# Deformable convolution on one core: halves of the first places, scales by DMA, and ScalarE weighting one of four neighbours

## The chip, the cores and the metric

The kernel runs on one core of a Trainium2 chip. The metric is the device time of one execution in microseconds (us). A core has five engines that run their own instruction streams and meet through semaphores: TensorE (PE, with its weight loads PEld), VectorE (DVE), ScalarE (ACT), GpSimd (POOL) and SyncE (SP, which here only issues DMAs).

## The reference

Four "metaformer" layers follow each other on x of shape (4, 128, 64, 64): each is a convolution-like mixer on a normalised x, added to x, and then a token mixer, added again. The change touches one of these eight steps, the mixer of layer 1: a modulated deformable 3x3 convolution. Cut to that:

```python
off  = conv2d(xn, w_off, b_off)                 # xn: x normalised over channels; 2 offsets per tap
mask = sigmoid(conv2d(xn, w_mod, b_mod))        # 9 taps
py, px = h + ky + dy, w + kx + dx               # where tap (ky, kx) of pixel (h, w) looks
y0, x0 = floor(py), floor(px); wy, wx = py - y0, px - x0
v00, v01, v10, v11 = xn at (y0,x0), (y0,x0+1), (y0+1,x0), (y0+1,x0+1)   # zero outside the image
sampled = (v00*(1-wy)*(1-wx) + v01*(1-wy)*wx + v10*wy*(1-wx) + v11*wy*wx) * mask
x = x + einsum('bckhw,ock->bohw', sampled, weight) + bias
```

## The kernel before

x stays in SBUF for the whole kernel as `xs`, 128 channels on the partitions, 4096 pixels per image (batch). An image is 8 chunks of 512 pixels, each 4 tiles of 128. The stage of interest is `deformable`, between the recurrence of layer 0 and the expert choice of layer 1.

Two taps of the nine (`HATS`) are computed without gathering, by hat functions (`hats`, whose steps lay work on every engine except GpSimd; `fold` prepares its matrices). The other seven (`BY_ASK`) gather. For each chunk and tap the four tiles are done in two pairs, so a chunk is 14 pairs, an image 112 and the stage 448. `taken` serves a pair: two indirect DMAs on GpSimd (L998) bring, for each of 128 pixels, the four neighbours' 128 channels (512 floats) from a table in DRAM into a buffer `dcn_g` (8 buffers); then one VectorE product (L1006) multiplies all of it, 1024 columns, by the weights. The weights lie in PSUM as `near_w`, copied there once a chunk (L1160). `joined` lets TensorE transpose the four weighted neighbours of a tile into the same PSUM columns, so that they add up: eight transposes a pair (L1015). `turn_back` copies the result to SBUF on ScalarE (L1120), `convolve` multiplies it by the tap's weights (L1127), and `finish` adds the chunk to `xs` (L1135).

Before an image can gather it needs its table and its places, which `plan(b)` prepares: the pixels are centred (L753, L756), their variances found (L759, L765), the reciprocal deviations made (`inverted`, L777), and each chunk is scaled (`scaled`: a matmul L792 spreads a row of deviations over the partitions, L801 multiplies). `turned` transposes the normalised rows and writes them to the table by SP DMAs (L818, L820, L827, L829). `offsets` convolves for offsets and mask, two halves of an image (L840, L849, L858). `places` turns them into indices (L915 to L944) and weights (L953 to L978) for the whole image, 288 columns a partition.

The order on TensorE, ScalarE, VectorE and GpSimd is the order of the program text (`manual_schedule`); each engine runs its stream in order. `plan` is a generator. For image 0 it runs to its end before the first gather. For image b+1 it is the side work of image b: every `step`, one per pair, advances it by one `yield`, every fifth step by two; what is left at the end of an image is run out before the next begins. `at(lag, ...)` defers work by so many steps: a pair's joins come two steps after its product.

Of the kernel before, what the change touches and what calls it, by code (L numbers as in the profile page):

```python
# [10 lines left out]

# [6 lines left out]
F32 = mybir.dt.float32  # L18
# [10 lines left out]
P = 128  # L29
# [563 lines left out]
class Sampling:  # L593
# [8 lines left out]
    def __init__(self, net, one, dram):  # L602
# [6 lines left out]
        self.tables = [dram.tile([SIDE * SIDE + 1, 2, P], F32, name=f"dcn_table{b}") for b in range(B)]  # L609
        zero = one.tile([SIDE + 1, 2 * P], F32, name="dcn_zero")  # L610
# [84 lines left out]
def deformable(net, sampling):  # L695
# [19 lines left out]
    with ExitStack() as ctx:  # L715
# [5 lines left out]
        far = one.tile([P, B + 1], F32, name="dcn_far")  # L721
# [14 lines left out]
        def plan(b):  # L736
# [4 lines left out]
            def bank(tag="pd" if b else "pt"):  # L741
                return ps.tile([P, CH], F32, name=f"dcn_{tag}", tag=tag, bufs=BANKS[tag])
# [45 lines left out]

            def scaled(c):
                rows = slice(32 * (c % 4), 32 * (c % 4) + 32)  # L790
                pb = bank()
                nc.tensor.matmul(  # L792
                    pb,
                    net.ident[rows, rows.start : rows.start + 1].to_broadcast([32, P]),
                    rstds[c // 4][rows],
                    start=True,
                    stop=True,
                )
                yield
                d = inside(c)  # L800
                nc.vector.tensor_mul(d, d, as_shape(pb, d))  # L801
                yield
# [75 lines left out]
            for c in half:  # L878
                yield from scaled(c)
            if b == 0:  # L880
                yield from abreast(
                    one_by_one(*(turned(c) for c in half)),
                    one_by_one(inverted(1), *(scaled(4 + c) for c in half)),
                )
                yield from abreast(
                    one_by_one(*(turned(4 + c) for c in half)),
                    one_by_one(offsets(0), offsets(1), places(b, off)),
                )
                return
            yield from turned(0)  # L890
            yield from turned(1)
            yield from inverted(1)
            yield from turned(2)
            yield from turned(3)
            for c in half:
                yield from scaled(4 + c)
# [6 lines left out]
            yield from places(b, off)  # L903

        def places(b, off):

            frac, row = [], new("row")
            hat = sb.tile([P, NT, NH, PICKED], F32, name="dcn_hat", tag="dcn_hat", bufs=1)
            apart = sb.tile([P, NT, NH, 1], F32, name="dcn_apart", tag="dcn_apart", bufs=1)
            pieces = sb.tile([P, NT, NH * PICKED, 3], BF16, name="dcn_pieces", tag="dcn_pieces")  # L910
            at = slice(H0, H0 + NH)
            for axis in range(2):
                pos, low, lowi, over = new("pos"), new("low"), new("lowi", I32), new("over")
                frac.append(new(f"frac{axis}"))
                nc.vector.tensor_add(pos, grids[axis], off[:, :, axis : 18 : 2])  # L915
                if axis == 0:
                    nc.vector.tensor_sub(apart[:, :, :, 0], pos[:, :, at], grids[0][:, :, at])
                    yield
                    nc.vector.tensor_reduce(
                        far[:, b : b + 1],  # L920
                        apart.rearrange("p t k o -> p (t k o)"),
                        AX.X,
                        ALU.max,
                        apply_absolute_value=True,
                    )
                else:
                    nc.vector.tensor_copy(hat[:, :, :, 0], pos[:, :, at])
                nc.vector.tensor_scalar(pos, pos, -1.0, float(H), op0=ALU.max, op1=ALU.min)
                yield

                nc.vector.tensor_copy(lowi, pos)
                nc.vector.tensor_copy(low, lowi)
                yield
                nc.vector.tensor_tensor(over, low, pos, ALU.is_gt)
                nc.vector.tensor_sub(low, low, over)
                yield
                nc.vector.tensor_sub(frac[axis], pos, low)
                if axis == 0:
                    nc.vector.tensor_scalar(row, low, float(SIDE), float(SIDE + 1), op0=ALU.mult, op1=ALU.add)
                else:  # L940
                    nc.vector.tensor_add(row, row, low)
                yield
            idx = new("idx", I32)
            nc.vector.tensor_copy(idx, row)  # L944
            ly, lx = frac
            mask, lo, hi = new("pos"), new("low"), new("over")
            w = new("w")
# [4 lines left out]
            shape = [P, NT, NH, PICKED - 1]  # L952
# [25 lines left out]
            nc.vector.tensor_mul(wq[1], hi, lx)  # L978
            made[b] = (sampling.squares(tables[b]), idx, w, pieces, turns[b])
# [11 lines left out]
        near_w = ps.tile([P, 2, Q4, KK, 4], F32, name="dcn_near_w", bufs=1)  # L991

        def taken(rows, idx, c, k, i):


            g = sb.tile([P, 2, 4 * P], F32, name="dcn_g", tag="g", bufs=GATHERED)
            for t in range(2):
                nc.gpsimd.indirect_dma_start(  # L998
                    out=g[:, t, :],
                    out_offset=None,  # L1000
                    in_=rows,
                    in_offset=bass.IndirectOffsetOnAxis(ap=idx[:, Q4 * c + i + t, k : k + 1], axis=0),
                )
            near = g.rearrange("p t (q c) -> p t q c", c=P)
            by = near_w[:, c % 2, i : i + 2, k, :].unsqueeze(3).to_broadcast([P, 2, 4, P])
            nc.vector.tensor_mul(near, near, by)  # L1006
            return near

        def joined(pt, i, near):

            if i == 0:
                pt[0] = ps.tile([P, CH], F32, name="dcn_pt", tag="pt", bufs=BANKS["pt"])
            for t in range(2):
                for q in range(4):
                    nc.tensor.matmul(  # L1015
                        pt[0][:, (i + t) * P : (i + t + 1) * P],
                        near[:, t, q, :],
                        net.ident,
                        is_transpose=True,
                        start=i + t + q == 0,  # L1020
                        stop=i + t + q == 6,
                        skip_group_check=True,
                    )
# [79 lines left out]
        with tc.manual_schedule(engines=ORDERED):  # L1103
# [44 lines left out]
            for b in range(B):  # L1148
                for _ in side:
                    pass  # L1150
                side = plan(b + 1) if b + 1 < B else iter(())
# [7 lines left out]
                for c in range(NCH):  # L1159
                    nc.vector.tensor_copy(near_w[:, c % 2], w[:, Q4 * c : Q4 * c + Q4])  # L1160
                    po = {}
                    busy.append(hats(b, c, po, pieces, turned))
                    if c == 2:
                        keep(b, idx, w)
                    if b == 0 and c < B:
                        nc.sync.dma_start(sampling.kept[c].rearrange("c p t -> p c t"), as_chunks(net.xs[:, c, :]))
                    for k in BY_ASK:
                        pt = {}
                        for i in range(0, 4, 2):
                            at(2, joined, pt, i, taken(rows, idx, c, k, i))  # L1170
                            if i:
                                at(4, turn_back, k, pt, po, b, c)
                            step()
            while later:
                step()
            nc.vector.tensor_reduce(far[:, B : B + 1], far[:, 0:B], AX.X, ALU.max)
            pt = ps.tile([P, CH], F32, name="dcn_pt", tag="pt", bufs=BANKS["pt"])
            nc.tensor.transpose(pt[0:1, 0:P], far[:, B : B + 1], net.ident)
# [1453 lines left out]
```

## Time and profile before

| | |
|---|---|
| median of 3 executions | 6042.37 us (6040.1 to 6043.02) |
| the profiled execution | 6034.38 us, its span 6032.6 us |
| mean granted TensorE clock | 0.975 |
| busy over the span | PE 5684.2, DVE 4380.3, ACT 3365.4, POOL 2057.2 us |
| first and last start of a gather (L998) | 1310.9 and 2445.4 us |
| gathers | 896, 851.3 us busy |

A row of a group reads: line, engine, operation, tiles out<-in, shapes, count | busy us, mean ns of one | idle time of the engine just before them, and what ended it. In a table of windows each engine has its busy time and, in brackets, its instructions; PEclk is the granted clock, DMA the busy share of the 16 DMA engines. In a timeline the columns are the start and the duration in us, and in square brackets the idle time before.

### The profile page before, as it was taken

To read this page: it belongs to the slowest core of one execution; us is meant where nothing else is said; L and a number is where in the kernel's file an instruction comes from. 1 tells how busy PE (TensorE), PEld (TensorE's weight loads), DVE (VectorE), ACT (ScalarE), POOL (GpSimd) and SP (SyncE) were. 2 spreads that over 40 slices of the span, in tenths; PEclk is the share of its full clock that TensorE was granted. 3 is DMA by queue.
4 is the path that set the end of the run, shared out by engine and by line. 5 is a ranking of instruction groups with operands and counts; after the bars stand their busy time and mean duration, and the time that the engine had idled before them with its cause. 6 is when DMAs were issued, how large, how long until landed. Compare 5 with 4: busy or idle time off the path is not lost. (4 is left out here: it accounts for less than half of the span.)

```text
span 6032.6 us, 97814 instructions
## 1 busy us (share of the span) xinstructions
PE 5684.2 (94%) x39896; PEld 2250.6 (37%) x39927; DVE 4380.3 (73%) x4783; ACT 3365.4 (56%) x4213; POOL 2057.2 (34%) x2015
## 2 busy tenths in 40 slices
PE   8999999889999988879979999999999999999799
PEld 2222222346667766433333222322232223222233
DVE  6888887456767676456446888888888888888666
ACT  4444444333323322521336888888888888999421
POOL 3898897027777777200010111111111111111000
PEclk9999999989999999979989999999999999999899
DMA  6434432057777777550274666656665666666200
GB/s 215 98 74 90 89 76 47 1 150 231 217 229 217 228 221 210 167 183 0 88 266 111 133 155 146 138 130 154 146 141 128 151 148 142 133 131 131 60 25 27
DMA packets 273274, 818.39 MB, mean 136 GB/s; under 512 B 42644, under 2 KB 100392, under 8 KB 226728
## 3 DMA queue, kind: packets, MB, share of 16 engines
q0 software_dynamic: 109568, 505.75, 35.2%
q1 hardware_dynamic: 163240, 306.20, 17.5%
q8 instruction: 320, 5.24, 0.4%
q14 instruction: 146, 1.20, 0.1%
HBM read 416.71 MB, written 93.13 MB: 85 GB/s over the span
## 5 line engine op out<-in xcount | busy, mean ns | idle before, releaser
L2035 ACT ACTIVATE att_ex<-att_sc,att_shift 128x1024 f32<-128x1024 f32 x2048 | 2141.8, 1111 | 281.3 <-PE att_sc L2031 165.1
L2066 DVE TENSOR_TENSOR att_dve<-att_dve,att_ex 128x2048 f32<-128x2048 f32 x704 | 1631.5, 2317 | 154.0 <-ACT att_ex L2035 129.2
L2031 PE MATMUL att_sc<-att_q,att_k 32*128 32x512 f32 x8192 | 1280.8, 640 | 0.0
L2047 PE MATMUL att_pv<-att_ex,att_vals 128*32 128x512 f32 x8192 | 1092.2, 605 | 0.0
L998 POOL DMA_INDIRECT dcn_g<-dcn_table,dcn_idx x896 | 851.3, 950 | 354.3 <-issue 150.8
L412 DVE SCALAR_TENSOR_TENSOR inv_prod<-inv_pk,bspan,inv_seen 128x512 f32<-128x512 f32 (+1 forms) x1120 | 774.5, 743 | 141.4 <-PE inv_pk L399 141.0
L410 POOL TENSOR_TENSOR inv_prod<-inv_seen,inv_prod 128x512 f32<-128x512 f32 (+1 forms) x672 | 837.5, 1273 | 95.2 <-ACT inv_prod L409 95.2
L2064 POOL DMA_DIRECT2D att_dma<-att_ex x224 | 192.5, 859 | 1965.1 <-ACT att_ex L2035 1738.6
L409 ACT ACTIVATE inv_prod<-inv_pk,bspan 128x512 f32<-128x512 f32 (+1 forms) x672 | 436.1, 682 | 504.9 <-PE inv_pk L399 493.7
L2031 PEld LDWEIGHTS att_sc<-att_q,att_k 32*128 32x128 f32 x8192 | 423.5, 183 | 656.5 <-issue 416.8
L1006 DVE TENSOR_TENSOR dcn_g<-dcn_g,dcn_near_w 128x1024 f32<-128x1024 f32 x448 | 538.9, 1214 | 164.9 <-DMA dcn_g<-dcn_table,dcn_idx 153.4
L399 PE MATMUL inv_pk<-inv_red,wtap 32*96 32x512 f32 (+1 forms) x3584 | 512.1, 637 | 7.3 <-DVE wtap L377 7.3
L1015 PE MATMUL dcn_pt<-ident,dcn_g 128*128 128x128 f32 x3584 | 472.9, 276 | 34.0 <-ACT dcn_st L1120 16.4
L1015 PEld LDWEIGHTS dcn_pt<-ident,dcn_g 128*128 128x128 f32 x3584 | 419.1, 142 | 206.9 <-issue 116.1
L421 PE MATMUL inv_out<-inv_prod,inv_fold 96*32 96x512 f32 (+1 forms) x3584 | 478.6, 606 | 8.5 <-DVE xs L429 8.5
L2047 PEld LDWEIGHTS att_pv<-att_ex,att_vals 128*32 128x32 f32 x8192 | 161.8, 108 | 752.2 <-issue 727.0
L399 PEld LDWEIGHTS inv_pk<-inv_red,wtap 32*96 32x96 f32 (+1 forms) x3584 | 131.9, 171 | 386.2 <-DVE inv_prod L412 362.5
L1034 ACT ACTIVATE dcn_fold<-dcn_pf,dcn_turn 128x256 f32<-128x256 f32 x128 | 60.2, 473 | 366.0 <-PE dcn_pf L1030 366.0
L1120 ACT COPY dcn_st<-dcn_pt 128x512 f32<-128x512 f32 x224 | 129.9, 580 | 241.0 <-PE dcn_pt L1015 241.0
L1127 PE MATMUL dcn_out<-dcn_st,dcn_wk 128*128 128x512 f32 x448 | 236.0, 609 | 25.0 <-DVE xs L1135 23.1
L2536 PE MATMUL top_po<-top_xg,top_we 128*128 128x512 f32 x512 | 233.3, 599 | 0.0
L1054 DVE TENSOR_TENSOR dcn_square<-dcn_hx,dcn_by 128x512 f32<-128x512 f32 x192 | 130.0, 677 | 115.4 <-PE dcn_by L1040 75.5
(442 smaller groups left out, 5358.1 us busy)
## 6 DMA issues: line engine op xcount, KB each, us to landing
att_dma<-att_ex POOLq DMA_DIRECT2D x224, 1024.0 KB, 7.0
inv_seen<-inv_image SPq DMA_DIRECT2D x256, 266.0 KB, 9.1
moe_w<-in_L_ffn_weight SPq DMA_DIRECT2D x64, 1024.0 KB, 14.2
att_dma<-att_ex SPq DMA_DIRECT2D x32, 1024.0 KB, 9.0
att_dve<-att_dma POOLq DMA_DIRECT2D x32, 1024.0 KB
moe_table<-moe_xt SPq DMA_DIRECT2D x64, 288.0 KB, 2.8
dcn_table<-dcn_xt SPq DMA_DIRECT2D x32, 512.0 KB, 4.8
dcn_g<-dcn_table,dcn_idx POOLq DMA_INDIRECT x896, 3.7
```

Of the source, the lines that this page charges most:

```text
L399: nc.tensor.matmul(pk[0:m], wtap[half][rg, i, blk], red[rg, h * CH : (h + 1) * CH], start=True, stop=True)
L409: nc.scalar.activation(prod[0:m, h], pk[0:m], AF.Identity, bias=by)
L410: nc.gpsimd.tensor_mul(of, view, of)
L412: nc.vector.scalar_tensor_tensor(out=of, in0=as_shape(pk[0:m], of), scalar=by, in1=view, op0=ALU.add, op1=ALU.mult)
L421: nc.tensor.matmul(po[CR * blk : CR * (blk + 1), h, :], fold[0:m], prod[0:m, h, :], start=unit == 0, stop=unit == UNITS - 1,)
L998: nc.gpsimd.indirect_dma_start(out=g[:, t, :], out_offset=None, in_=rows, in_offset=bass.IndirectOffsetOnAxis(ap=idx[:, Q4 * c + i + t, k ...
L1006: nc.vector.tensor_mul(near, near, by)
L1015: nc.tensor.matmul(pt[0][:, (i + t) * P : (i + t + 1) * P], near[:, t, q, :], net.ident, is_transpose=True, start=i + t + q == 0, stop=i + ...
L2031: nc.tensor.matmul(pes[h // 2][:, h % 2, :], ks[r, t * P : (t + 1) * P], q[r], start=True, stop=True)
L2035: nc.scalar.activation(ex[:, 2 * two : 2 * two + 2, :], pes[two], AF.Exp, bias=shifts[g][:, two : two + 1],)
L2047: nc.tensor.matmul(block["pv"][r], vals[:, t, r], ex[:, h, :], start=t == 0, stop=t == NT - 1)
L2066: nc.vector.tensor_add(block[who], block[who], ex)
```

## The change

- Image 0's places are made in halves. The first half (chunks 0 to 3) follows the first half of the offsets; the second offsets and the second half of the places become side work of image 0, ahead of `plan(1)`, and must be done by chunk 3. `places` takes a slice `part` and a column of `far` for it; `places_held` makes the tiles.
- For images 1 to 3 the row of deviations is written to DRAM (`spread_out`) and read back spread over 128 partitions (`way`), in place of the matmul in `scaled`. The order of `plan` changes: `inverted(1)` comes first, the second half is scaled earlier.
- Of a tile's four neighbours, the first is weighted by ScalarE into one of three slots of PSUM, which lie in one bank with `near_w`. VectorE multiplies the last two neighbours as before (512 columns), and then, in `added`, forms second x weight + slot, per tile. Three transposes a tile remain. `near_w` holds two weights instead of four, once instead of twice.

The core of the diff (places' statements, which only gain the slices, are left out):

```diff
+            front = [b == 0]
+            def bank(tag=None):
+                tag = tag or ("pt" if front[0] else "pd")
...
+            def spread_out(h):
+                nc.sync.dma_start(sampling.spread[b][4 * h : 4 * h + 4, :], rstds[h][0:P:32])
+                yield
+                for c in range(4 * h, 4 * h + 2):
+                    way(c)
+                    yield
+            def way(c):
+                by = ways[c] = sb.tile([P, CH], F32, name="dcn_way", tag="ln_sq", bufs=4)
+                nc.sync.dma_start(by, sampling.spread[b][c : c + 1, :].to_broadcast([P, CH]))
             def scaled(c):
+                if b:
+                    pb = ways.pop(c)
+                else:
...
                 yield
                 d = inside(c)
                 nc.vector.tensor_mul(d, d, as_shape(pb, d))
+                if b and c % 4 < 2:
+                    way(c + 2)
                 yield
...
             yield from inverted(0)
             if b == 0:
...
-                    one_by_one(offsets(0), offsets(1), places(b, off)),
+                    one_by_one(offsets(0), places(b, off, held, slice(0, NT // 2), 0)),
                 )
+                front[0] = False
+                rest.append(one_by_one(offsets(1), places(b, off, held, slice(NT // 2, NT), B)))
                 return
+            yield from spread_out(0)
+            yield from inverted(1)
+            for c in half:
+                yield from scaled(c)
+            yield from spread_out(1)
             yield from turned(0)
             yield from turned(1)
-            yield from inverted(1)
+            for c in half:
+                yield from scaled(4 + c)
             yield from turned(2)
...
-        near_w = ps.tile([P, 2, Q4, KK, 4], F32, name="dcn_near_w", bufs=1)
+        shared = ps.tile([P, CH], F32, name="dcn_near_w", bufs=1)
+        near_w = shared[:, 0 : Q4 * KK * 2].rearrange("p (i k q) -> p i k q", k=KK, q=2)
+        first = shared[:, P:CH].rearrange("p (s c) -> p s c", c=P)
+        taking = [0]
...
-            by = near_w[:, c % 2, i : i + 2, k, :].unsqueeze(3).to_broadcast([P, 2, 4, P])
-            nc.vector.tensor_mul(near, near, by)
+            slots = [(taking[0] + t) % 3 for t in range(2)]
+            taking[0] += 2
+            for t in range(2):
+                nc.scalar.activation(
+                    first[:, slots[t], :], near[:, t, 0, :], AF.Copy, scale=w[:, Q4 * c + i + t, k, 0:1]
+                )
+            by = near_w[:, i : i + 2, k, :].unsqueeze(3).to_broadcast([P, 2, 2, P])
+            nc.vector.tensor_mul(near[:, :, 2:], near[:, :, 2:], by)
+            at(1, added, w, c, k, i, near, slots)
             return near
+        def added(w, c, k, i, near, slots):
+            for t in range(2):
+                nc.vector.scalar_tensor_tensor(
+                    out=near[:, t, 1, :], in0=near[:, t, 1, :], scalar=w[:, Q4 * c + i + t, k, 1:2],
+                    in1=first[:, slots[t], :], op0=ALU.mult, op1=ALU.add,
+                )
         def joined(pt, i, near):
-                for q in range(4):
+                for q in range(1, 4):
...
-                side = plan(b + 1) if b + 1 < B else iter(())
+                side = chain(rest[0] if b == 0 else (), plan(b + 1) if b + 1 < B else ())
...
                 for c in range(NCH):
-                    nc.vector.tensor_copy(near_w[:, c % 2], w[:, Q4 * c : Q4 * c + Q4])
+                    if b == 0 and c == NCH // 2 - 1:
+                        for _ in rest[0]:
+                            pass
+                    nc.vector.tensor_copy(near_w, w[:, Q4 * c : Q4 * c + Q4, :, 2:])
```

## The prediction

> **What bounds the kernel now.** The change touches only the deformable convolution, so I read the page for its groups, then its four batches as windows, then the wait list of the line that gathers, then the timelines of GpSimd and of the prelude. Four windows, cut at the first gather of each batch; batches 1 and 3:
>
> ```profile
> core 0: us, PE busy (x) PEld busy (x) DVE busy (x) ACT busy (x) POOL busy (x), PEclk, DMA share, GB/s
> ...
> 1596.00:1882.00 286.00, 272.37 (x1822) 200.25 (x1829) 199.95 (x248) 90.21 (x169) 212.59 (x225) 0.99 0.75 224
> ...
> 2166.00:2446.00 280.00, 241.19 (x1568) 189.52 (x1575) 173.34 (x177) 70.26 (x129) 211.78 (x225) 0.96 0.71 211
> ```
>
> TensorE looks like the limit, 95% busy in batch 1. But batch 3, which has no next batch to prepare and leaves TensorE at 86%, is only 6 us shorter. GpSimd, 75% busy in both, is the engine to look at. The gathering line, with its idle time by releaser (us, times), and its timeline:
>
> ```profile
> L998 POOL DMA_INDIRECT dcn_g<-dcn_table,dcn_idx x896: 940/946/1294, 1310.9 to 2445.4; - x180
> ...
>   issue: 150.8, 495
>   DVE dcn_idx L944: 70.1, 1
> ...
>   DVE dcn_g L1006: 33.1, 90
>   PE dcn_pt L1015: 27.9, 73
> ```
>
> ```profile
> 2201.69 0.95 POOL L998 DMA_INDIRECT dcn_g<-dcn_table,dcn_idx  x1 [0.30 <-issue]
> 2202.94 0.95 POOL L998 DMA_INDIRECT dcn_g<-dcn_table,dcn_idx  x1 [0.30 <-issue]
> ```
>
> Each gather takes 0.946 us and 0.304 us of gap, also where it waits for nothing ("issue": 150.8/495 = 0.305). That is a period of 1.25 us, 2.50 us for a pair, and nothing on GpSimd shortens it. 896 gathers at 1.251 us are 1120.9 us; from the first start to the last the trace has 1134.5 us for 895 periods. The surplus is 15.1 us and can be named: waits for VectorE's product 33.1 - 90 x 0.304 = 5.7; for TensorE's joins 27.9 - 73 x 0.304 = 5.7; gathers longer than the median 851.3 (page) - 896 x 0.946 = 3.7. So GpSimd's pace bounds the stage, and TensorE adds some 11 us. The other two places where this stage can give or lose time are its start, 70.1 us of GpSimd waiting for the first index, and the seams between batches, which cost nothing now (1595.13 to 1596.38, one period).
>
> **The change, part by part.**
>
> *First places in halves.* The prelude on VectorE:
>
> ```profile
> 1291.90 0.80 DVE L858 COPY dcn_off<-dcn_pt 128x108 f32<-128x108 f32 x4 [15.66 <-PE dcn_pt L853]
> 1302.36 0.80 DVE L858 COPY dcn_off<-dcn_pt 128x108 f32<-128x108 f32 x4 [9.66 <-PE dcn_pt L853]
> 1303.20 0.46 DVE L915 TENSOR_TENSOR dcn_pos<-dcn_at,dcn_off 128x288 f32<-128x288 f32 x1
> ...
> 1310.32 0.31 DVE L944 CAST dcn_idx<-dcn_row 128x288 int32<-128x288 f32 x1
> ```
>
> The first half needs only the offsets ready at 1292.7. The chain L915 to L944 takes 7.43 us at 288 columns. At 144 its nine two-input operations save some 0.15 us each (0.46 at 288 against 0.23 at 64 columns), its eight casts and scalings 0.075, three small ones 0.1 together: 5.4 us. Index at 1298.2. The gather also waits for the table. Its last writes are issued at 1295.4 and 1296.0, after transposes that stood behind the second offsets; without those the last copy (1294.75) comes some 1.8 us earlier, so writes at 1293.6 and 1294.2, landing 4.5 to 4.8 us later at 1298.1 to 1299. First gather 1298.7 instead of 1310.9: **-12.2** (bounds -11 and -13). The other half of the places (some 12 us of VectorE) and the second offsets move beside the gathers of chunks 0 to 2, where VectorE is 71% busy; exposed, they would cost their 12 us.
>
> *The seam that this opens.* The side work advances 1.2 yields a step, 134 in the 112 steps of a batch. A plan had 123 yields, and was done 9 steps before its batch ended. It now has 129 (the DMAs of the scales add 6), and batch 0 first spends 31 on the deferred half: 160. The last 26, which are places(1) whole, turned(7) and part of turned(6), are flushed after batch 0's last step; the built program has them on VectorE between the last product of batch 0 and the first of batch 1. GpSimd then waits for index 1. With T the start of batch 0's last gather: landing T+3.7 (median of L998), ScalarE, product and joins some 1.8, index chain 7.4, so T+13. By the table: four transpose-and-copy rounds through the one bank "pd", some 1.15 us each (0.58 copy plus TensorE and hops), from T+5 to T+9.6, issue 0.6 twice, landing 4.5: T+15. Against T+1.25 now: **+13.5** (bounds +11.5 and +16). The rest of the places (9 us) is covered by the sixteen gathers that the eight buffers allow, 20 us. Batches 1 and 2 keep 5 yields in hand: no stall.
>
> *Three joins, and ScalarE's weighting.* TensorE loses 896 of 3584 transposes. They start 0.109 us apart within a pair, so that is 98 us of TensorE, and 24 scale matmuls of two passes more; but 11.4 us is all that TensorE and VectorE cost GpSimd now. If that goes and 3.7 us of lengthened gathers stay: **-10** taken (bounds -15 and 0).
>
> What replaces it is a chain. Nothing in the trace has ScalarE writing a bank that VectorE reads, so prices come from the nearest forms:
>
> ```profile
> L1034 ACT ACTIVATE dcn_fold<-dcn_pf,dcn_turn 128x256 f32<-128x256 f32 x128 | 60.2, 473 | 366.0 <-PE dcn_pf L1030 366.0
> ...
> L1479 ACT COPY moe_raw<-moe_acc 128x128 f32<-128x128 f32 x4 | 1.1, 265 | 22.4 <-PE moe_acc L1477 22.4
> ```
>
> ```profile
> L1135 DVE SCALAR_TENSOR_TENSOR xs<-dcn_out,dcn_bias,xs 128x512 f32<-128x512 f32 x32 | 23.8, 743 | 3.0 <-PE dcn_out L1127 3.0
> ...
> L2424 DVE SCALAR_TENSOR_TENSOR top_rest<-top_hit,top_lg 128x128 f32<-128x128 f32 x8 | 2.3, 282 | 0.0
> ```
>
> A 128x128 weighting lies between 0.265 and 0.473 us; a scale column adds 0.1 (0.684 for L409 against 0.580 for L1120, both 512 wide), so 0.366. A 128x128 fused multiply-add lies between 0.282 and 0.34 (the column adds 0.06: 0.743 against 0.677 of L1054). The half-width product is L1054's form, 0.68, or 0.60 to the next start. In the built program ScalarE's first weighting of a pair waits for VectorE's last addition of the pair before, its second waits for its first, and VectorE's product waits for the second. So a round is serial: 2 x 0.366 + 0.03, hop 0.03, 0.60 + 0.25 + 0.32, hop 0.06 = **2.02 us** (bounds 1.75 and 2.45), under GpSimd's 2.50.
>
> Work queued behind these waits adds to it, per chunk of 14 rounds: the chain rowt, "by" matmul, hx on ScalarE, 1.0; folds that wait for TensorE in the same step, 4 x 0.3; steps in which a square and a side operation together exceed the 0.8 us in which VectorE waits for ScalarE, 3 x 0.5; likewise ScalarE, 2 x 0.4. That is 4.5 on 28.3: 32.8 us against GpSimd's 35.0. So the chain is covered by 6%; if it were not, each 0.1 us of round costs 45 us.
>
> The Trainium skill ("PSUM — Partial Sum Buffer", section "PSUM bank collisions raise a hardware error") speaks against this part: two engines must be kept off one bank by semaphore, even at different addresses. No row of this trace shows it; with slots and near_w in separate banks the round would be the larger of the engines' shares, some 1.2 us.
>
> *Scales by DMA.* 24 transfers of 256 KB and 6 small ones on SP, where table writes land in 4.8 us; each is asked for at least 8 us ahead: 0 (bound +3 if VectorE waits).
>
> *Places beside gathers.* GpSimd's long gathers (1.29 us at 1851.65) fall where L963 to L978 run: 3.7 us in three batches. Half a set is added and one goes into the seam: 0. The skill ("SBUF — State Buffer", "Who interferes with whom") says that copies, casts and tensor_scalar in two-port mode block descriptor generation for the whole instruction; by it the added half, 15 such operations of 0.2 us, would cost 3 us.
>
> *Tail.* The last pair now runs two engines in turn: +0.8.
>
> **Sum:** -12.2 + 13.5 - 10 + 0.8 = -8 us. The profiled execution took 6034.4 us (span 6032.6), 8.0 under the median of 6042.4; carried to the median, **6034 us**.
>
> **Rivals.** *A: the ScalarE-VectorE chain sets the pace* (slower). Place: the shared bank, every pair. It decides from a bare round of 2.18 us, since 14 x 2.18 + 4.5 = 35. At 2.35 (weighting 0.45, joins 0.34 without overlap) a chunk takes 37.4 us: 24 chunks of batches 0 to 2 x 2.4 = 58, none in batch 3, less the 11.4 of surplus whose place it takes, plus 2.1 of prelude, seam and tail: 49, some 6091; just over the point, 6045. For it: both engines stand in program order behind TensorE's results (ScalarE now idles 366 us before folds, harmlessly). Against it: the sum above, and eight buffers that even out single late rounds. *B: the seam is cheaper and all surplus goes* (faster): +11.5, -15, -12.2, +0.8 = -15, 6027. For it: TensorE, at 95%, is what every wait of GpSimd leads to. *C: the change does not do what it says:* the built program has six transposes a pair and half-width places, so not weighed beyond 1 in 50.
>
> **How the numbers follow.** Forecast 0.48 (its own range 6029 to 6046), A 0.34, B 0.16, C 0.02. A measurement of this kernel tells about 0.2% from no change, 12 us. Faster by more than that: 0.14 of B and 0.02 of the forecast. Slower: 0.30 of A, and 0.04 of the forecast with a dearer seam. Within: the rest, 0.50. The range runs from B's end, 6025, to the middle of A, 6072.
>
> **What would show it.** Right: first gather near 1299; a hole of some 14 us in GpSimd at the first seam only; 1.25 us between gathers in all batches; TensorE near 80%. Wrong: GpSimd waiting for ScalarE or VectorE in every pair (A), weightings over 0.45 us, VectorE idle before its product on ScalarE while gathers have landed, no hole at the seam (B), or holes at later seams.

## The result, and the profile after

The changed kernel takes 6062.59 us (6062.08 to 6071.24, 6 executions) against 6041.48 us (6037.6 to 6044.36) of the kernel before on the same chip: ratio 1.0042, 95% interval 1.0032 to 1.0053. It is slower by 21 us, where the forecast was 8 us faster; 6062 lies inside the stated range, but on the side that the forecast had not taken. The profiled executions are 27.7 us apart (6062.08 and 6034.38), and the gathering stage holds nearly all of it.

The batches of after as windows, from the first gather of each to the next seam:

```profile
core 0: us, PE busy (x) PEld busy (x) DVE busy (x) ACT busy (x) POOL busy (x), PEclk, DMA share, GB/s
1606.94:1896.28 289.34, 244.80 (x1490) 166.57 (x1498) 197.33 (x460) 160.48 (x378) 213.72 (x224) 0.95 0.76 228
1896.28:2191.89 295.61, 252.84 (x1574) 173.36 (x1581) 199.34 (x469) 166.84 (x392) 213.06 (x224) 0.97 0.75 223
2191.89:2471.04 279.15, 223.86 (x1370) 162.88 (x1376) 177.64 (x416) 151.15 (x359) 211.24 (x223) 0.98 0.73 212
```

TensorE fell from 95% to 85% in batches 1 and 2, as intended, and yet these got longer, 289 and 296 us against 286 and 284. Batch 3, which has no side work, did not. What GpSimd waited for (us, times):

```profile
L1044 POOL DMA_INDIRECT dcn_g<-dcn_table,dcn_idx x896: 940/946/1420, 1296.6 to 2471.0; - x180
...
  issue: 125.6, 407
...
  ACT dcn_near_w L1054: 34.7, 101
  DMA dcn_g<-dcn_table,dcn_idx: 30.8, 101
  DVE dcn_hat L1007: 26.1, 3
  DVE dcn_g L1064: 19.9, 60
  ACT dcn_st L1184: 16.0, 31
  DVE dcn_square L1118: 15.3, 25
```

Ordinary gaps of 0.30 us ("issue") fell from 495 to 407. ScalarE's weighting, which is not in the kernel before, now ends 101 of GpSimd's gaps, as many as the gathers' own landings, though all but 4 of its 34.7 us are the ordinary gap (34.7 - 101 x 0.304); and one wait of 25.5 us (in the row of L1007) is new. ScalarE and VectorE on the pairs, as groups:

```profile
L1054 ACT ACTIVATE dcn_near_w<-dcn_g,dcn_w 128x128 f32<-128x128 f32 x896 | 331.6, 370 | 328.3 <-DVE dcn_g L1064 232.7 <-DVE dcn_near_w L1227 44.2 <-DMA dcn_g<-dcn_table,dcn_idx 33.5
L1058 DVE TENSOR_TENSOR dcn_g<-dcn_g,dcn_near_w 128x512 f32<-128x512 f32 x448 | 307.1, 686 | 377.6 <-ACT dcn_near_w L1054 374.1 <-DMA dcn_g<-dcn_table,dcn_idx 1.7 <-PE dcn_by L1104 0.9
L1064 DVE SCALAR_TENSOR_TENSOR dcn_g<-dcn_g,dcn_w,dcn_near_w 128x128 f32<-128x128 f32 x896 | 268.3, 341 | 0.0
```

Read them as a pair: the product waits 374 us for the weighting and the weighting 233 us for VectorE's addition, while the gathers (DMA) hold up ScalarE for 33.5 us and the product for 1.7. Timelines of two rounds, where nothing else intervenes:

```profile
2198.78 0.77 ACT L1054 ACTIVATE dcn_near_w<-dcn_g,dcn_w 128x128 f32<-128x128 f32 x2 [0.76 <-DVE dcn_g L1064]
2200.83 0.78 ACT L1054 ACTIVATE dcn_near_w<-dcn_g,dcn_w 128x128 f32<-128x128 f32 x2 [1.27 <-DVE dcn_g L1064]
...
2197.54 0.69 DVE L1058 TENSOR_TENSOR dcn_g<-dcn_g,dcn_near_w 128x512 f32<-128x512 f32 x1 [0.84 <-ACT dcn_near_w L1054]
2198.15 0.60 DVE L1064 SCALAR_TENSOR_TENSOR dcn_g<-dcn_g,dcn_w,dcn_near_w 128x128 f32<-128x128 f32 x2
2199.59 0.69 DVE L1058 TENSOR_TENSOR dcn_g<-dcn_g,dcn_near_w 128x512 f32<-128x512 f32 x1 [0.84 <-ACT dcn_near_w L1054]
```

One engine stands while the other works; the bare round is 2200.83 - 2198.78 = 2.05 us. The first seam, on GpSimd and on ScalarE and SP ahead of it:

```profile
1580.50 0.94 POOL L1044 DMA_INDIRECT dcn_g<-dcn_table,dcn_idx  x1 [0.30 <-issue]
1606.94 1.01 POOL L1044 DMA_INDIRECT dcn_g<-dcn_table,dcn_idx  x1 [25.50 <-DVE dcn_hat L1007]
...
1591.17 0.69 ACT L872 ACTIVATE dcn_om<-dcn_pv,dcn_boff 128x512 f32<-128x512 f32 x1 [4.00 <-PE dcn_pv L863]
...
1601.71 0.64 SPq L852 DMA_DIRECT2D dcn_table<-dcn_xt  x1
...
1602.86 0.31 DVE L987 CAST dcn_idx<-dcn_row 128x288 int32<-128x288 f32 x1
...
1595.96 0.60 PE L841 MATMUL dcn_pd<-ident,dcn_pad 128*64 128x128 f32 x4
```

The hole, GpSimd's wait at this seam, is 25.2 us beyond one period. L1007, the named releaser, is a coincidence: the index was ready at 1603.2 (L987), and what came last is, by elimination, the table, whose last write was issued at 1601.71. The trace has no landing for this write; the gather starts 5.2 us after its issue, and the last but one of the run with the halves alone landed 4.5 us after its own. It was late because TensorE was in arrears, that is, behind with work asked for earlier. Two windows:

```profile
1570.00:1580.00 10.00, 10.00 (x72) 5.20 (x71) 8.60 (x20) 4.70 (x13) 7.36 (x8) 1.00 0.79 229
1580.00:1590.00 10.00, 10.00 (x72) 5.76 (x70) 5.66 (x14) 3.30 (x9) 1.14 (x2) 1.00 0.25 77
```

From 1570 to 1590 TensorE is busy without a gap. From 1568.8 on, 72 matmuls of image 1's second offsets (L863) lie among the pairs' joins; ScalarE waited for these until 1591.17, and the transposes that fill the table began at 1595.96, T+15.5 (T: start of the batch's last gather).

To compare runs I split each profile in the same way. "Start" is from the stage's first matmul to its first gather; "seams" what the three seams take beyond 1.251 us; "surplus" the sum over all other gather periods of their time beyond 1.251 us, split into gathers that took longer than 0.946 us (GpSimd's busy time less 896 x 0.946 = 847.6) and the rest, which are waits.

| us | start | seams | waits | longer gathers | ratio to before, interval |
|---|---|---|---|---|---|
| before | 71.6 | 0 | 11.2 | 3.7 | |
| after | 58.3 | 25.8 | 23.8 | 5.1 | 1.0042 (1.0032 to 1.0053) |
| halves alone | 58.3 | 20.5 | 16.0 | 2.6 | 1.0008 (0.9999 to 1.0017) |
| weighting alone | 69.2 | 0 | 40.1 | 4.0 | 1.0034 (1.0022 to 1.0046) |
| scales by DMA alone | 69.1 | 0 | 4.3 | 9.9 | 0.9997 (0.9988 to 1.0006) |
| after, weighting in place | 58.2 | 18.5 | 0.6 | 16.5 | 1.0011 (1.0002 to 1.0020) |

Before to after: -13.3 (start) + 25.8 + 12.6 + 1.4 = 26.5, with about 1 us in the stages around it. The start differs by 2.5 us among runs that do not change it (69.1 to 71.6), so the halves bring 11 to 13 us.

### The profile page after: what moved, and what is told of

Read it like the earlier page. It is cut to its first block, busy times and chain, and to the rows that moved or that the text cites. A ratio compares the mean times of both kernels' runs of the same rounds, so it can differ in the third digit from the quotient of the medians.

```text
span 6060.3 us, 99541 instructions
## 1 busy us (share of the span) xinstructions
PE 5610.9 (93%) x38952; PEld 2143.2 (35%) x38983; DVE 4385.8 (72%) x5714; ACT 3676.0 (61%) x5112; POOL 2059.1 (34%) x2015
## 5 line engine op out<-in xcount | busy, mean ns | idle before, releaser
L1044 POOL DMA_INDIRECT dcn_g<-dcn_table,dcn_idx x896 | 852.7, 952 | 379.6 <-issue 125.6
L1058 DVE TENSOR_TENSOR dcn_g<-dcn_g,dcn_near_w 128x512 f32<-128x512 f32 x448 | 307.1, 686 | 377.6 <-ACT dcn_near_w L1054 374.1
L1054 ACT ACTIVATE dcn_near_w<-dcn_g,dcn_w 128x128 f32<-128x128 f32 x896 | 331.6, 370 | 328.3 <-DVE dcn_g L1064 232.7
L1079 PE MATMUL dcn_pt<-ident,dcn_g 128*128 128x128 f32 x2688 | 385.6, 281 | 93.9 <-ACT dcn_st L1184 38.2
L1079 PEld LDWEIGHTS dcn_pt<-ident,dcn_g 128*128 128x128 f32 x2688 | 316.8, 144 | 325.0 <-DVE dcn_g L1064 126.0
L1064 DVE SCALAR_TENSOR_TENSOR dcn_g<-dcn_g,dcn_w,dcn_near_w 128x128 f32<-128x128 f32 x896 | 268.3, 341 | 0.0
L2584 DVE TENSOR_TENSOR top_xg<-top_d,top_pw 128x512 f32<-128x512 f32 x256 | 158.2, 680 | 61.7 <-PE top_pw L2574 61.7
```

Source lines behind the costliest of these rows:

```text
L1044: nc.gpsimd.indirect_dma_start(out=g[:, t, :], out_offset=None, in_=rows, in_offset=bass.IndirectOffsetOnAxis(ap=idx[:, Q4 * c + i + t, k ...
L1079: nc.tensor.matmul(pt[0][:, (i + t) * P : (i + t + 1) * P], near[:, t, q, :], net.ident, is_transpose=True, start=i + t + q == 1, stop=i + ...
```

## The experiments

The five rows of the first table beside before itself ran on chips where the kernel before takes 6037 to 6042 us. All later runs fell on four other chips, where it takes 6249 to 6265 us and the engines of this stage pause for reasons that the trace does not name (last section); there a run is compared only with runs on the same chip. The code cuts below show the lines that matter, with "..." where lines are left out.

**The parts alone.** Halves only (places in halves, before's weighting and scales; the cut is against the changed kernel):

```diff
-                if b:
-                    pb = ways.pop(c)
-                else:
+                if True:
...
-            by = near_w[:, i : i + 2, k, :].unsqueeze(3).to_broadcast([P, 2, 2, P])
-            nc.vector.tensor_mul(near[:, :, 2:], near[:, :, 2:], by)
-            at(1, added, w, c, k, i, near, slots)
+            by = near_w[:, c % 2, i : i + 2, k, :].unsqueeze(3).to_broadcast([P, 2, 4, P])
+            nc.vector.tensor_mul(near, near, by)
...
-                for q in range(1, 4):
+                for q in range(4):
```

> The kernel before with the halves of the first places alone (no weighting on ScalarE, no scales by DMA). 31 yields are put ahead of plan(1)'s 123 where 134 fit, so 20 are flushed at the first seam: the places and the last piece of turned(7). Theory (the hole is as long as VectorE's and TensorE's arrears at the seam plus the index chain): the first gather starts 12 to 15 us earlier; before's arrears at the end of batch 0 are 11.7 us from the issue of a pair to its product, so the last product is at T+10.5 (T: start of batch 0's last gather), the index 7.4 us later, a hole of 17 to 20 us; surplus of batches 1 to 3 as before. Sum +2 to +6 against the kernel before. Rival (the prediction's count of the seam: no arrears): hole 13 us, sum -2.

Measured: ratio 1.0008, +5 us by the ratio (-1 to +10 by its interval), +9 by the medians. The seam on GpSimd:

```profile
1584.37 0.95 POOL L1035 DMA_INDIRECT dcn_g<-dcn_table,dcn_idx  x1 [0.30 <-issue]
1606.13 1.10 POOL L1035 DMA_INDIRECT dcn_g<-dcn_table,dcn_idx  x1 [20.81 <-DVE dcn_pieces L999]
```

Hole 20.5 us (17 to 20 expected), waits 16. The last product of batch 0 ends at T+8.4 (1592.73, T = 1584.37), the index is ready at T+15.7, but the last table write was issued at T+16.8, and the hole ended at T+21.8. So in the profile the halves cost more at the seam and in waits (20.5 + 4.8 us) than the 11 to 13 that they save at the start, without any ScalarE weighting.

Weighting only (against the kernel before):

```diff
-            nc.vector.tensor_mul(near, near, by)
...
+                nc.scalar.activation(
+                    first[:, slots[t], :], near[:, t, 0, :], AF.Copy, scale=w[:, Q4 * c + i + t, k, 0:1]
+                )
...
+            nc.vector.tensor_mul(near[:, :, 2:], near[:, :, 2:], by)
+            at(1, added, w, c, k, i, near, slots)
...
-                for q in range(4):
+                for q in range(1, 4):
```

> The kernel before with the weighting on ScalarE and three joins alone (whole places, scales by matmul, plan of 123 yields that fits a batch). Theory (the shared PSUM bank makes a pair one serial round of ScalarE and VectorE, which can't catch up after a burst of side work): no hole, first gather at 1311, but the sum of gather periods over 1.25 us is 25 to 45 us instead of 15, most of it in batches 1 and 2; +10 to +30 us. Rival 1 (the surplus of the changed kernel comes from the new order of plan and from its transfers): surplus falls to 5 or less because TensorE has 98 us less to do, -10 us. Rival 2 (as the prediction had it: round covered): -10.

Measured: 1.0034, +22 us by the medians (6058.96 and 6036.95). No hole, waits 40.1 us, of which batches 1 and 2 hold most:

```profile
L1001 POOL DMA_INDIRECT dcn_g<-dcn_table,dcn_idx x896: 940/946/1364, 1308.8 to 2472.5; - x180
...
  ACT dcn_near_w L1011: 38.1, 84
  DVE dcn_g L1021: 25.7, 81
```

Both rivals fall: this part alone costs as much as the whole change did (+21), and it gains nothing from TensorE's relief.

Scales only (places whole, VectorE weights all four; against the changed kernel, whose scales stay):

```diff
-                    one_by_one(offsets(0), places(b, off, held, slice(0, NT // 2), 0)),
+                    one_by_one(offsets(0), offsets(1), places(b, off, places_held(b), slice(0, NT), b)),
...
-            nc.vector.tensor_mul(near[:, :, 2:], near[:, :, 2:], by)
-            at(1, added, w, c, k, i, near, slots)
+            by = near_w[:, c % 2, i : i + 2, k, :].unsqueeze(3).to_broadcast([P, 2, 4, P])
+            nc.vector.tensor_mul(near, near, by)
...
-                for q in range(1, 4):
+                for q in range(4):
```

> The kernel before with the scales by DMA and the new order of plan alone (whole places, VectorE weights all four, four joins). 129 yields of 134 that fit. Theory (shared bank): 0 (-3 to +4), no hole at any seam, surplus near before's 15. Rival (the order of plan and its transfers make the surplus of the changed kernel): +10 to +15 in batches 0 to 2.

Measured: 0.9997. Waits fall to 4.3 us, and gathers get 6.2 us longer; the two cancel. Of the 6.2 us, 3.3 lie in the 32 gathers that overlap one of the 24 scalings (1.049 us in the mean; 0.945 in before, where the scale came from PSUM). The rest is not explained: in the changed kernel, which has the same scalings, all gathers together are only 1.4 us longer than in before.

**The shared bank.** The changed kernel, with ScalarE writing back into the gather's own buffer:

```diff
-                    first[:, slots[t], :], near[:, t, 0, :], AF.Copy, scale=w[:, Q4 * c + i + t, k, 0:1]
+                    near[:, t, 0, :], near[:, t, 0, :], AF.Copy, scale=w[:, Q4 * c + i + t, k, 0:1]
...
-                    in1=first[:, slots[t], :],
+                    in1=near[:, t, 0, :],
```

> The changed kernel, but ScalarE writes its weighted neighbour back into dcn_g in SBUF and VectorE's fused addition reads it there; near_w is alone in its PSUM bank, three joins stay. VectorE's product then waits for the gather alone and ScalarE no longer waits for the pair before. Theory (shared bank): arrears at the end of a chunk fall from 15 to 20 us to under 10, a chunk's products recover at 30 us or less instead of 34, surplus over 1.25 us falls from 30 to 12 or less, the hole shrinks from 26 to 15 to 18; 15 to 30 us under the changed kernel, near 6035. Rival (engine shares, not the bank: ScalarE and VectorE have too much queued behind TensorE): surplus and hole stay within 5 us of the changed kernel's, 6058 to 6063.

Measured: 1.0011, 6043.42 us, against 1.0042: 19 us under the changed kernel by the ratios, and 8 over the 6035 expected. Groups of this run:

```profile
L1042 POOL DMA_INDIRECT dcn_g<-dcn_table,dcn_idx x896 | 864.1, 964 | 348.8 <-issue 132.9 <-DVE dcn_pieces L1005 56.7 <-DMA dcn_g<-dcn_table,dcn_idx 43.9
L1050 ACT ACTIVATE dcn_g<-dcn_g,dcn_w 128x128 f32<-128x128 f32 x896 | 333.3, 397 | 306.1 <-DMA dcn_g<-dcn_table,dcn_idx 273.1 <-DVE dcn_g L1060 12.3 <-DVE dcn_g L1054 4.3
L1054 DVE TENSOR_TENSOR dcn_g<-dcn_g,dcn_near_w 128x512 f32<-128x512 f32 x448 | 305.3, 682 | 218.8 <-DMA dcn_g<-dcn_table,dcn_idx 209.4 <-PE dcn_pt L1075 4.8 <-PE dcn_by L1100 2.7
```

ScalarE and VectorE now wait for gathers (273 and 209 us) and hardly for each other (12.3 and 4.3 us in the row of L1050), and GpSimd's own waits fall from 23.8 to 0.6 us. That is the step that the theory asked for. But the gathers take 11.4 us longer (864.1 against 852.7), so the whole surplus is 17, not under 12, and the hole is 18.5, half a microsecond over what was expected: the transposes of the last table rows begin at T+8.8 (1596.05, T = 1587.25) instead of T+15.5, again after 20 us of TensorE without a gap. So the slots in the shared bank made some 7 us of the hole; the other 18.5 come with the flushed side work, behind TensorE's queue. Two things differ between these kernels, the bank and the number of places to write to (three slots, or eight gather buffers), and this run does not tell them apart.

**The side work in image 0 made faster**, so that its 160 yields fit:

```diff
-                if n % 5 == 0:
+                if n % (2 if b == 0 else 5) == 0:
```

> The changed kernel, but the side work of image 0 advances by two yields every second step (168 in 112 steps) instead of every fifth, so that the 160 are done before the first seam. Theory (the hole and the shared bank are two separate costs): no hole, -25; but the hole is also where a batch's arrears are paid off, so batch 1 now starts with 12 to 16 us of arrears and its surplus rises from 8.5 towards the 21 that the weighting alone had; net -10 to -18 against the changed kernel, +4 to +12 against the kernel before. Rival (the hole is the whole trouble): -25 or more against the changed kernel, level with the kernel before or under it.

> The kernel before with the halves of the first places, and two yields every second step for image 0 (154 needed, 168 there). Theory (an opened seam is what ate the gain of the halves): first gather 13 us earlier, no hole, surplus 15 to 20: -8 to -14 against the kernel before. Rival (the denser side work puts TensorE and VectorE so far behind that GpSimd waits in batch 0 instead): surplus of batch 0 over 12, 0 to -5.

> The changed kernel with both mended: ScalarE's weighting in place in dcn_g, and the faster side work in image 0. Theory: no hole (-18 against the version in place), surplus 17 to 20 of which 13 are gathers that take longer: -8 to -12 against the kernel before. Rival (the arrears that the hole paid off come back as waits): level with the kernel before.

> The halves, the scales by DMA with the new order of plan, and the faster side work in image 0, without ScalarE's weighting. Theory: as the halves with the faster side work, since the scales by DMA alone were level: -9 to -15 against the kernel before, the best of the four or level with the halves alone. Rival (gathers lengthened by the scales from SBUF, 6 us busier in the run of the scales alone): 3 to 6 us over the halves with the faster side work.

These ran on the first of the chips on which the kernel before is slow (6258.99). Ratios: after with the pace 1.0077, halves with the pace 1.0004 (0.9995 to 1.0013), in place with the pace 0.9967 (0.9952 to 0.9982), halves and scales with the pace 0.9977 (0.9968 to 0.9986). The expectations were in microseconds of a chip without pauses and can't be held against these in size; by sign, after with the pace is slower than before, on the theory's side, the halves gained nothing, on their rival's, and in place with the pace gained more than was expected. That the scales by DMA, level alone, bring 12 us here beside the halves (6246.67 against 6258.64) is not explained. Three were run again on another chip, with the weighting in place alone as a fourth:

> The changed kernel with two yields every second step in image 0, again, since the first time the chip ran the kernel before 220 us slower. Theory (hole and shared bank are two costs, and the hole pays off arrears): no hole, surplus 38 to 50 instead of 29, -10 to -18 against the changed kernel, +4 to +12 against the kernel before. Rival (the hole is the whole trouble): level with the kernel before or under it.

> The halves of the first places with two yields every second step in image 0, again on another chip. Theory: first gather 13 us after the prelude's start earlier than before, no hole, surplus 15 to 20: -8 to -14 against the kernel before. Rival (denser side work makes GpSimd wait): surplus of batch 0 over 12, 0 to -5.

> The changed kernel with ScalarE's weighting in place in dcn_g and the faster side work in image 0, again on another chip. Theory: no hole, surplus 17 to 20, of which 13 are gathers that take longer: -8 to -12 against the kernel before. Rival (arrears come back as waits): level with it.

> The kernel before with ScalarE's weighting and three joins alone, but the weighted neighbour written back into dcn_g in SBUF instead of a slot in the bank of near_w. It differs from the run with the slots in nothing else. Theory (the shared bank makes the round serial): surplus 15 to 20 instead of 44, 13 of it lengthened gathers; 0 to +5 against the kernel before. Rival 1 (ScalarE's and VectorE's own work, whatever the bank): surplus near 44, +20. Rival 2 (the prediction: three joins take the waits for TensorE away, and nothing else happens): surplus under 6, -8 to -10.

This chip paused too (6248.62). Ratios 1.0064, 0.9984 (0.9974 to 0.9994: -9 us for the halves, at the theory's end this time), 0.9966, and for the weighting in place alone 0.9986 (0.9977 to 0.9995): -9 us, where the rival of ScalarE's and VectorE's own work wanted +20. The theory's 0 to +5 was missed as well, and -9 is what rival 2 asked for in time; its surplus under 6 us can't be read among the pauses. Then the changed kernel itself beside these:

> The changed kernel itself, unchanged, for the comparison with the three others on the same chip. On a chip without the stops: +20 to +25 against the kernel before. On one with them: theory (a serial round can't catch up after a stop, as after a burst of side work): the price of the bank grows with the number of stops; with some 40 of them +35 to +60. Rival (the price is a fixed 20 to 25 us of seam and round): +20 to +25 there too.

> The changed kernel with two yields every second step in image 0. Theory (the hole also pays off arrears): without stops 10 to 18 under the changed kernel of this call, not 25; with stops, where arrears never run out, 5 to 15 under it. Rival (the hole is a plain cost): 25 or more under it.

> Both mended: weighting in place, and two yields every second step in image 0. Theory: without stops no hole, surplus 15 to 20, 10 to 14 under the kernel before; with stops 20 to 25 under it, as twice before. Rival (arrears come back as waits without stops): level with the kernel before.

> The kernel before with ScalarE's weighting in place and three joins alone. Theory: without stops the waits fall from 11 us to under 3, the gathers lengthen by 10 to 13, so 0 to +4 against the kernel before; with stops 6 to 12 under it, as once before. Rival (ScalarE's and VectorE's own work sets the pace): without stops +15 to +22, as with the slots.

Measured with pauses (before 6265.43): after 1.0089 (1.0073 to 1.0104), +58 us; after with the pace 1.0060, 20 us under it; in place with the pace 0.9965 (0.9953 to 0.9978), -22; weighting in place alone 0.9980, -12. The price of the change is larger where the engines pause, 58 us instead of 21, as the theory said and the fixed price did not; that it grows with the number of pauses rests on this chip and the one of the last runs. The hole of 23.8 us was worth 20, between the two expectations, and in the profiles the surplus did not rise without it (281 against 291): that a hole pays off arrears is not shown.

**Which coupling of the bank.** The weighting alone, and the same with VectorE's product reading its weights from SBUF, so that the slots have the bank for themselves:

```diff
-            by = near_w[:, i : i + 2, k, :].unsqueeze(3).to_broadcast([P, 2, 2, P])
+            by = w[:, Q4 * c + i : Q4 * c + i + 2, k, 2:].unsqueeze(3).to_broadcast([P, 2, 2, P])
```

> The weighting on ScalarE into slots beside near_w and three joins alone, as in the first call. Theory (serial round, which can't catch up): without stops +18 to +25 against the kernel before as before; with stops +35 to +50, since the changed kernel had +58 there with its hole. Rival (a fixed price): +20 to +25 with stops too.

> The same, but VectorE's product reads its two weights from w in SBUF, and the slots have the bank for themselves: the product no longer waits for ScalarE, while ScalarE still waits for the addition of the pair before. The round is then two weightings 0.75, two additions 0.60 and hops, about 1.45 us, with the product beside the weightings. Theory (the length of the serial round is what counts): surplus without lengthened gathers under 5 us without stops; with stops as the weighting in place, 5 to 12 under the kernel before; gathers lengthen by 10 to 20 us as the product now reads two operands from SBUF. Rival (any wait of ScalarE for VectorE is enough): as with the shared bank, +20 without stops, +35 to +50 with.

Measured with pauses (before 6249.34): 1.0067, +38 us, and 1.0035, +22. The gathers of the two runs, as groups:

```profile
L1001 POOL DMA_INDIRECT dcn_g<-dcn_table,dcn_idx x896 | 853.1, 952 | 602.4 <-issue 278.5 <-ACT dcn_near_w L1011 89.0 <-DVE dcn_idx L944 67.6
```

```profile
L1000 POOL DMA_INDIRECT dcn_g<-dcn_table,dcn_idx x896 | 919.8, 1027 | 515.3 <-issue 216.9 <-DVE dcn_idx L944 70.1 <-ACT dcn_near_w L1010 64.8
```

The product now waits for ScalarE nowhere. GpSimd's idle time falls by 87 us (602.4 to 515.3), and its gathers take 67 us longer; by the medians 15 us are gained (6286.91 to 6271.83). Some of the 87 is only that a slower gatherer waits less, so the run shows a gain, and not how much of it the shorter round makes; reading both operands of the product from SBUF is no way to get it. ScalarE still waits 178 us for VectorE's additions; how much of the remaining +22 is this coupling of the slots stays open. The time lies between theory and rival.

## Why the prediction was wrong

- **The prices per instruction and the start were right.** Weighting 0.370 us (0.366 said), addition 0.341 (0.282 to 0.34), bare round 2.05 in the median of the undisturbed ones (2.02), three joins, TensorE at 80 to 86%. First gather at 1296.6 (1298.7 said); of the 14.3 us that it came earlier 1.0 lies before the stage.
- **The term that failed first: "work queued behind these waits", 4.5 us a chunk, 32.8 in all, "covered by 6%".** In batch 2 of after the 112 products took 297.2 us from the first to the first of batch 3, 37.1 a chunk, with GpSimd held at the buffers' limit (a pair's product up to 22 us after its first gather); the first two chunks of batch 3, without side work, took 31.7 and 31.9. Over eight chunks of the bare 28.7 (14 x 2.05) that is 68 us queued instead of 36, 8.4 a chunk. In place, with the same side work on every engine, the products of batch 2 took 282.0 us, so it is the coupling through the slots that queues it. The windows tell where it comes from: batch 2 has 21.7 us more VectorE work and 15.7 more ScalarE work than batch 3, 37 of the 43 us between 297.2 and 8 x 31.8. I had let side work hide in the 0.8 us in which VectorE waits for ScalarE and counted only what exceeds it. I read this so: in a serial round each engine's side work mostly delays the other too, so both shares count nearly in full. The sums fit, but no run isolates it. That is rival A, with the right place, but its deciding point, a bare round of 2.18 us, rested on the same 4.5; with 8.4 queued it lies at (35.0 - 8.4) / 14 = 1.90.
- **"-10: TensorE's and VectorE's waits go"** was right without the bank (11.2 to 0.6 us in place) and wrong with it (23.8). Even in place it brought nothing on the chip without pauses, since "places beside gathers 0" and "scales by DMA 0" left out longer gathers: +12.8 us in place, of which the gathers that overlap a scaling hold 5.6.
- **The seam, "+13.5 (bounds +11.5 and +16)", measured 25.2.** The sum began with the last pair's joins at T+5.5, as if all engines stood level with GpSimd at the end of a batch. In before's own trace the products of batch 0's last chunk began up to 11.7 us after their gathers, which this term left out. In after the table's transposes began at T+15.5 instead of T+5, 1.30 us apart instead of 1.15, and the gather began 4.6 us after the last write's issue ended (4.5 said); that is +10.5 and +0.6 of the 11.7 missing. The halves alone, with 20 flushed yields, still had a hole of 20.5.
- **How far each step missed.** The sum said -8, and the profiles are 26.5 us apart in this stage. Of the 34.5 us between them 24 lie in the waits and longer gathers (-10 said, +12.6 and +1.4 measured) and 12.3 in the seams (+13.5 said, +25.8 measured); the start came 1.1 better than said, and the 0.8 of the tail is not in this split.
- **The Trainium skill.** "PSUM — Partial Sum Buffer", section "PSUM bank collisions raise a hardware error", asks that two engines be kept off one bank; the prediction put a round of 1.2 us beside 2.02 for separate banks. No run shows the error itself, but the price of the waits that keep ScalarE and VectorE apart here: 2.05 us a round, and +38 us with the slots against -9 and -12 in place, on three chips with pauses. "SBUF — State Buffer", section "Who interferes with whom", says besides the sentence on two-port modes that I used that a VectorE instruction with two SBUF inputs contends with a GpSimd instruction that reads SBUF. The runs agree: with the product's second operand in PSUM a gather takes 0.952 us in the mean, with both in SBUF 1.027, and the 487 gathers that overlap a product take 1.090, the others 0.951. The same section infers that a `tensor_tensor` leaves the making of a DMA's descriptors alone; for these gathers the measurement says otherwise.
- **Which version is best.** In place with the faster side work: 0.9967, 0.9966 and 0.9965 on three chips, 21 to 24 us under the kernel before, all with pauses. On a chip without them it was not run; from the row in place and its hole of 18.5 us I estimate 6043 - 18 = 6025 there, 12 under before.

## What to carry to other kernels

When a producer and a consumer on two engines share one buffer in turn, add up everything that both engines have in their queues, side work included, and compare that sum with the pace that has to be kept: here a bare round of 2.05 us against a pace of 2.50 was not enough, once 8.4 us a chunk were queued. At a point where a queue is run out (a seam, a flush), start the count from how far each engine is behind there, which a table of "work begun less data asked for" shows in the trace of before. A named releaser that has long been done, as L1007 at the seam, sends one to the transfer that landed last.

## What was unexpected in the hardware

Longer gathers: moving operands of VectorE from PSUM to SBUF lengthened GpSimd's gathers by 3 us (24 scalings, by the gathers that overlap them), 5 to 11 us (896 additions, in four pairs of runs; there ScalarE's output moves to SBUF too) and 67 us (448 products of 512 columns), though all of these are two-operand forms.

Pauses: on four chips the stage took some 200 us longer, in the kernel before too (by the medians), at 0.952 to 0.967 mean granted clock of the span instead of 0.967 to 0.978, while the stages after it kept their time (3574 to 3591 us from the last update of `xs` in this stage, against 3575 to 3582). There the profiles have idle time put down to "remote", of which over 0.6 us before has one (1.2 us) in this stage and after none. TensorE and ScalarE in the halves with the faster side work:

```profile
2331.39 1.03 PE L1067 MATMUL dcn_pf<-dcn_cw,xs 128*128 128x256 f32 x4
2336.21 1.22 PE L1067 MATMUL dcn_pf<-dcn_cw,xs 128*128 128x256 f32 x2 [3.79 <-ACT dcn_fold L1071]
```

```profile
2335.69 0.84 ACT L1071 ACTIVATE dcn_fold<-dcn_pf,dcn_turn 128x256 f32<-128x256 f32 x2 [8.50 <-remote]
```

ScalarE's fold begins more than 3 us after its matmuls (all of the first four ended at 2332.42), and nothing in the trace holds it. ScalarE has 23 to 44 such waits of over 0.6 us a run, 109 to 243 us. What causes them stays open. That the coupling through the slots is dearer on these chips is what the ratios above show (the change +58 us instead of +21, the weighting alone +38 instead of +22); that the pauses make it so is the theory.
